# Layer 2's last norm of each pair applied to rows as they lie, and one stream's last statistics made by ScalarE

## The chip, the cores and the metric

One core of a Trainium2 chip. The metric is device microseconds of one execution. The kernel before takes 1713.87 us, median of three executions (1713.86 to 1713.9).

## What is computed

x has 8 items of 512 tokens by 512 features, all float32. The reference, cut to what matters:

```python
def _mingru(x, Wz, bz, Wh, bh):                     # Wz = Wh = ctx_1024[i], bz = bh = cond_1024[i]
    z = sigmoid(einsum('bsi,hi->bsh', x, Wz) + bz)
    h_tilde = tanh(einsum('bsi,hi->bsh', x, Wh) + bh)
    a = clip(1.0 - z, 1e-8, 1 - 1e-8)
    return _linear_scan(a, z * h_tilde)             # h[t] = a[t] * h[t-1] + z[t] * h_tilde[t]

def _stack(x, ...):
    h = x
    for i in range(4):                              # layers 0 to 3
        h_new = _mingru(h, ...)
        if i > 0: h_new = h_new + h
        h = _layernorm(h_new, gamma, beta)          # over the 512 features
    return h

x = x + concat(_stack(norm(x)), flip(_stack(flip(norm(x))))) @ fusion_W.T + fusion_b
x = x + layernorm(gelu(norm(x) @ ternary(W_fc).T)) @ ternary(W_proj).T
```

Each item has two directions, forward and backward, so that there are 16 streams of four layers. Both directions use the same weights; the backward one differs in that its scan runs from the end.

## The kernel before

**Layout.** The state of a stream, `state[s]`, is a tile of 128 partitions (features of one chunk) by 4 chunks by 512 tokens: features lie on the partitions, tokens along the row. That is what the gate matmuls and the scan along tokens want. The layernorm is over features, that is over partitions. So `norm` (line 340) turns each of the four token tiles with four transposes on TensorE into a PSUM bank `pt` (`turned`, line 316; pool `ps_t`, two banks), where a token has its features along the row. `stats` (line 168) makes mean and variance on VectorE (`bn_stats`, `bn_aggr`, and two small instructions for `ve`, the variance plus epsilon, and `nmu`, minus the mean), and GpSimd takes the power -0.5 (`rs`, line 178). ScalarE writes the normalised tokens `tok` from the bank (`nmr` and `tok`, lines 188 and 189). Then `back` (line 320) turns the four chunks back, four transposes each, into a bank `pf` (pool `ps_f`, two banks), and ScalarE writes the chunk into the state with gamma as scale and beta as bias (line 331).

Layer 3 has no turning back: its norm is folded into the fusion weights, and `norm_last` (line 354) makes only the statistics: four transposes into `pt`, `bn_stats`, `bn_aggr`, `ve`, and the power into `rsv`. The fusion scales its two products by `rsv` (line 609).

**Order.** The order on every engine is the order in which the program is written (`manual_schedule`). It is made of slots (`slot`, line 439). A slot first issues its own work, mostly the eight matmul instructions of one output chunk of a layer, into one of four banks `u` (`gates`, line 457; two instructions per float32 matmul), followed by three activations on ScalarE for `a`, `t` and `z` (lines 479 to 481). Then it takes what is due of other streams: one piece from `turns` (the turning and its statistics), one from `backs` (the turning back), and one each from `xturns` and `xbacks` (`x_shares`; these serve the norm of the input of the next pair, whose last step `scale_x` makes four transposes into a `ps_f` bank `pr` and a ScalarE copy, and in the last pair the norm before the feed-forward part, whose transposes go to a `ps_f` bank `py`). Then come clamp, product and scan of the slot on VectorE (lines 485, 490, 494), the additions that are due ("resid": in layer 3 the sums of line 571, one a slot), and at the very end the closures that the pieces returned, in the order of the shares (`last`). A closure registered as "late" for a later slot is run there before the shares.

`Tokens` counts the four tiles of a norm; the turning back is ready one slot after the fourth tile was appended. `held` counts tiles of the `tok` pool in use; turns wait while it is 10.

**Pairs.** Items go in pairs. The four streams of a pair b are here called A = (b, 0), B = (b, 1), C = (b+1, 0) and D = (b+1, 1). Layers 1 to 3 run as A, B, C, D of layer 1, then of layer 2, then of layer 3, four slots each; then comes the fusion of the two items, between whose slots layer 0 of the next pair is put. D is the last stream whose layer 2 ends. In what follows slot n is counted from the first slot of D's layer 2: slots 0 to 3 are D's layer 2, 4 to 7 A's layer 3, 8 to 11 B's, 12 to 15 C's, 16 to 19 D's, and from 20 on the fusion and the next layer 0. By the pauses in the code D's turning falls into slots 5 to 8 and its turning back into slots 9 to 12. The sums of A's layer 3 are in slots 7 to 10 and of B's in 11 to 14. A's last statistics are in slots 12 to 15, B's in 16 to 19, C's from 20 and D's from 24. The input norm of the next pair's first item has its statistics in slots 4 to 7 and `pr` in slot 9, that of the second item in slots 12 to 15 and 17. In the last pair there is no next pair; the four `py` are there instead, one a slot, from the second slot after their fourth token tile.

After the 16 streams the feed-forward part runs over 16 hidden chunks of each item.

Of the kernel before, what the change touches and what calls it, by code (L numbers as in the profile page):

```python
# [9 lines left out]
F32 = mybir.dt.float32  # L10
F32R = mybir.dt.float32r
AF = mybir.ActivationFunctionType
ALU = mybir.AluOpType
# [3 lines left out]
P = 128  # L17
LN_EPS = 1e-5
# [6 lines left out]
def kernel(  # L25
# [26 lines left out]
    nc = tc.nc  # L52
    B, S, H = x.shape
    L = gru_wT.shape[0]
    F = fc_wT.shape[1]
    NC_ = H // P
    NT = S // P
# [7 lines left out]
    small = ctx.enter_context(tc.tile_pool(name="small", bufs=8))  # L65
    wpool = ctx.enter_context(tc.tile_pool(name="wts", bufs=1))
    hp = ctx.enter_context(tc.tile_pool(name="h", bufs=6))
    dram = ctx.enter_context(tc.tile_pool(name="x1", bufs=1, space=bass.MemoryType.DRAM))

    tokp = ctx.enter_context(tc.tile_pool(name="tok", bufs=TOK))  # L70
    xsp = ctx.enter_context(tc.tile_pool(name="xs", bufs=12))
    zp = ctx.enter_context(tc.tile_pool(name="z", bufs=ZT))
    ps_f = ctx.enter_context(tc.tile_pool(name="ps_f", bufs=2, space=PSUM))
# [18 lines left out]
    xs = {}  # L92
# [15 lines left out]
    gam = const.tile([P, NC_], F32, name="gam")  # L108
    bet = const.tile([P, NC_], F32, name="bet")
# [11 lines left out]
    for i in range(2):  # L121
# [3 lines left out]
        s = fusp.tile([P, P], F32R, name=f"fpick{i}")  # L125
# [36 lines left out]
    ident = const.tile([P, P], F32, name="ident")  # L162
    make_identity(nc, ident)
    mhalf = const.tile([P, 1], F32, name="mhalf")
    nc.vector.memset(mhalf, -0.5)
    ngb = const.tile([P, L, NC_], F32, name="ngb")

    def stats(src, name, rs=None, shift=True):

        st = small.tile([P, 6], F32, tag="st", name=f"st_{name}")  # L170
        nc.vector.bn_stats(st, src)  # L171
        mv = small.tile([P, 2], F32, tag="mv", name=f"mv_{name}")
        nc.vector.bn_aggr(mv, st)  # L173
        if rs is None:
            rs = small.tile([P, 1], F32, tag="rs", name=f"rs_{name}")
        ve = small.tile([P, 1], F32, tag="ve", name=f"ve_{name}")
        nc.vector.tensor_scalar(ve, mv[:, 1:2], LN_EPS, None, ALU.add)
        nc.gpsimd.tensor_tensor(rs, ve, mhalf, ALU.pow)  # L178
        if not shift:
            return rs, None  # L180
        nmu = small.tile([P, 1], F32, tag="nmu", name=f"nmu_{name}")
        nc.vector.tensor_scalar(nmu, mv[:, 0:1], -1.0, None, ALU.mult)  # L182
        return rs, nmu

    def normalise(dst, src, rs_nmu, name):
        rs, nmu = rs_nmu
        nmr = small.tile([P, 1], F32, tag="nmr", name=f"nmr_{name}")
        nc.scalar.activation(nmr, nmu, AF.Copy, scale=rs)
        nc.scalar.activation(dst, src, AF.Identity, bias=nmr, scale=rs)  # L189
# [39 lines left out]
    with rec:  # L229
# [7 lines left out]
        now = [0]  # L237
        state = {}
        rsv = {}
        turns, backs = [], []  # L240

        held = [0]
# [32 lines left out]
        zlive = [0]  # L275

        left = {}

        def queue(q, key, at, piece, go):
            left[key] = left.get(key, 0) + 1  # L280
            q.append((at, piece, key, go))
# [6 lines left out]
        def need(*keys):  # L288

            while any(left.get(k) for k in keys):  # L290
                slot(None, 2)

        def tokens(source, tok, rs, name):

            def go():
                src = source()
                found = stats(src, name, rs, tok is not None)
                if tok is None:
                    return lambda: None
                held[0] += 1  # L300

                def last():
                    tile_ = tokp.tile([P, H], F32, tag="tok", name=f"tok_{name}")
                    normalise(tile_, src, found, name)
                    tok.append(tile_)
                return last
            return go

        def turned(zs, t, name, frees=0):
            def source():  # L310
                if t == NT - 1:
                    zlive[0] -= frees
                spare = name.startswith("00_0") and t > 1
                pt = (ps_f if spare else ps_t).tile([P, H], F32, tag="pf" if spare else "pt", name=f"pt_{name}")
                for c in range(NC_):
                    nc.tensor.transpose(pt[:, ts(c, P)], zs[c][:, ts(t, P)], ident)  # L316
                return pt
            return source
# [35 lines left out]
        def norm_last(s, tag):  # L354
            rsv[s] = small.tile([P, NT], F32, tag="rsv", name=f"rsv_{tag}")
            zs = [state[s][:, c, :] for c in range(NC_)]
            for t in range(NT):
                queue(turns, s, now[0] + NC_ + 1, t, tokens(turned(zs, t, f"{tag}_{t}"), None, rsv[s][:, t : t + 1], f"{tag}_{t}"))

        rx, scale = {}, {}  # L360

        def scale_x(b):
# [9 lines left out]
                return last  # L372
            return go

        def second(b, t):

            def go():
                src, name = xs["n", b, t], f"x{b}_{t}"
                sm, nm, ss, ve = (small.tile([P, 1], F32, tag=k, name=f"{k}_{name}") for k in ("sm", "nm", "ss", "ve"))
                nc.scalar.activation(src, src, AF.Copy, accum_out=sm)  # L380
                nc.scalar.activation(nm, sm, AF.Copy, scale=-1.0 / H)
                nc.scalar.activation(src, src, AF.Square, bias=nm, accum_out=ss)

                def end():
                    nc.vector.tensor_scalar(ve, ss, 1.0 / H, LN_EPS, ALU.mult, ALU.add)
                    nc.gpsimd.tensor_tensor(rx[b][:, t : t + 1], ve, mhalf, ALU.pow)
                stages.append((now[0] + 1, "late", end))
                return None if now[0] or b else end
            return go
# [33 lines left out]
        stages = []  # L423
# [15 lines left out]
        def slot(work=None, cap=1, long=False):  # L439

            end = work() if work is not None else None
            due("factors")
            due("late")
            due("clamps")
            if long:
                due("scans")
            last = shares(cap) + x_shares()
            due("scans")
            if end is not None:
                end()  # L450
            due("resid")
            for f in last:
                if f is not None:
                    f()
            now[0] += 1

        def gates(h, l, o, name, scans):

            def work():
                u = ps_u.tile([P, S], F32, tag="u", name=f"u_{name}")  # L460
                for c in range(NC_):
                    nc.tensor.matmul(  # L462
                        u, lhsT=gw[l][:, c, ts(o, P)], rhs=h[:, c, :],
                        start=(c == 0), stop=(c == NC_ - 1),
                    )
                z = zp.tile([P, S], F32, tag="z", name=f"z_{name}")
                zlive[0] += 1
                a, t = factors(u, z, l, o, name)

                def end():  # L470
                    product(a, z, t)
                    scans(a, z)
                return end
            return work
# [17 lines left out]
        def scan(dst, a, z, backward):  # L492
            d = slice(None, None, -1) if backward else slice(None)
            nc.vector.tensor_tensor_scan(dst[:, d], a[:, d], z[:, d], 0.0, ALU.mult, ALU.add)  # L494
# [59 lines left out]
        def layer(s, l):  # L554
            while s not in state:
                slot(None, 2)
            need(s)
            zs = []
            h = state[s]
            for o in range(NC_):  # L560
                def scans(a, z, o=o):
                    scan(z, a, z, s[1] == 1)
                    zs.append(z)
                    if l < L - 1:
                        nc.vector.tensor_tensor(z, z, h[:, o, :], ALU.add)  # L565
                    elif o == NC_ - 1:

                        for c in range(NC_):
                            def sums(c=c):
                                zlive[0] -= 1  # L570
                                nc.vector.tensor_tensor(h[:, c, :], zs[c], h[:, c, :], ALU.add)
                            stages.append((now[0] + c, "resid", sums))
                slot(gates(h, l, o, f"{s[0]}{s[1]}_{l}_{o}", scans))

                if s[0] < 2 and (l == L - 1 or o % 2) and len(extra) > 2 * NW or s == (B - 1, 1) and l == L - 1:
                    pieces(1)
            now[0] -= 1
            if l < L - 1:
                norm(s, zs, f"{s[0]}{s[1]}_{l}", 2)
            else:  # L580
                norm_last(s, f"{s[0]}{s[1]}_{l}")
            now[0] += 1
# [165 lines left out]
        end = take(xturns)  # L748
# [94 lines left out]
    for i in range(2):  # L843
# [5 lines left out]
        s = const.tile([P, P], F32R, name=f"pick{i}")  # L849
# [137 lines left out]
    for j in range(ends):  # L987
        b, k = divmod(j, NF)
        late = []
# [22 lines left out]
        at = 12 if b == 0 else 8  # L1012
# [57 lines left out]
```

## Time and profile before

| | |
|---|---|
| median of three executions | 1713.87 us |
| the profiled execution | 1714.24 us |
| its span, first to last instruction | 1712.0 us |
| TensorE matmul / VectorE / ScalarE / GpSimd busy | 99% / 85% / 63% / 13% |
| granted TensorE clock | 1.000 |
| one transpose on TensorE, busy (line 325) | 273 ns, four of them start to start 0.44 us |
| eight matmul instructions of a chunk (line 462), start to start | 3.44 us |
| `bn_stats` from PSUM (line 171) | 693 ns |
| scan (line 494) | 1227 ns |
| `nmr` and `tok` on ScalarE (lines 188, 189) | 295 and 778 ns |
| affine from PSUM on ScalarE (line 331) | 786 ns |

Busy time of TensorE matmuls overlaps from one instruction to the next, and 99% says only that something is always in the array. What a step costs on TensorE is read from the starts of the instructions around it. Lines of the timeline give start, length, engine, line, operation and tiles; consecutive equal ones are merged, with their number at the end; in brackets is the idle time before and what ended it.

### The profile page before, as it was taken

The page shows a single profiled execution, that of the slowest core. Times are in us where ns is not written, and L with a number is a line of the kernel's source. Part 1 is how long each engine was busy: PE and PEld are TensorE (multiplying, and loading weights), DVE is VectorE, ACT ScalarE, POOL GpSimd, SP SyncE. Part 2 cuts the span into 40 slices and gives each one's busy share as a digit, 9 for nine tenths or more (in the row PEclk, how much of TensorE's full clock was granted, in tenths as well). Part 3 has the DMA queues.
Part 4 walks back from the last instruction along what each step waited for, and adds up shares of the span by engine and source line. Part 5 has one row for each costly group of instructions (what it writes and reads, how often), then busy time and mean ns, then how long its engine had stood idle before and what let it go on. Part 6 is the DMA issues. An engine that isn't in the chain of part 4 may idle for free.

```text
span 1712.0 us, 19766 instructions
## 1 busy us (share of the span) xinstructions
PE 1701.1 (99%) x6440; PEld 1042.4 (61%) x6440; DVE 1453.2 (85%) x2859; ACT 1074.6 (63%) x1858; POOL 222.3 (13%) x342
## 2 busy tenths in 40 slices
PE   9999999999999999999999999999999999999999
PEld 5455554555555455555545555554688888888887
DVE  7999989889998998999899899996568768768877
ACT  5898873468886246888524688860366566666654
POOL 3111111111111111111111111110000000000000
PEclk9999999999999999999999999999999999999999
DMA  8002231150000125000012200202201101100100
GB/s 271 19 25 81 99 93 37 65 193 1 1 19 13 56 68 191 1 1 19 13 56 69 104 21 29 74 1 99 74 1 50 50 0 50 49 19 31 50 19 31
DMA packets 46598, 91.74 MB, mean 54 GB/s; under 512 B 5280, under 2 KB 5536, under 8 KB 45472
## 3 DMA queue, kind: packets, MB, share of 16 engines
q1 hardware_dynamic: 45488, 88.78, 15.3%
q10 hardware_dynamic: 1008, 1.70, 0.3%
q8 instruction: 51, 0.84, 0.2%
q14 instruction: 51, 0.42, 0.1%
HBM read 65.30 MB, written 25.17 MB: 53 GB/s over the span
## 4 chain that ended last, share of the span: by engine, by line
PE 79%; DVE 16%; ACT 2%; issue 1%; DMA 1%; POOL 0%; DVEq 0%; ACTq 0%
PE u L462 28%; PE po L909 14%; PE ph L882 14%; PE pu L599 10%; PE pt L316 5%; DVE z L494 4%; PE pf L325 4%; PE u L511 4%; DVE st L171 2%; DVE z L490 2%; DVE a L485 1%; DVE z L565 1%; DVE zf L494 1%; PE py L214 1%; DVE mv L173 1%
## 5 line engine op out<-in xcount | busy, mean ns | idle before, releaser
L462 PE MATMUL u<-xT,gw 128*128 128x512 f32 x768 | 345.5, 593 | 0.0
L462 PE MATMUL u<-h,gw 128*128 128x512 f32 x768 | 345.5, 592 | 0.0
L494 DVE TENSOR_TENSOR_SCAN z<-a,z 128x512 f32<-128x512 f32 x224 | 274.9, 1227 | 7.6
L462 PEld LDWEIGHTS u<-xT,gw 128*128 128x128 f32 x768 | 138.6, 190 | 138.7 <-issue 136.8
L462 PEld LDWEIGHTS u<-h,gw 128*128 128x128 f32 x768 | 138.6, 190 | 138.2 <-issue 138.0
L479 ACT ACTIVATE a<-u,ngb 128x512 f32<-128x512 f32 x192 | 131.6, 685 | 139.6 <-PE u L462 139.1
L178 POOL TENSOR_TENSOR rs<-ve,mhalf 128x1 f32<-128x1 f32 x192 | 122.3, 637 | 679.8 <-DVE nmu L182 663.2
L171 DVE BATCH_NORM_STATS2 st<-pt 128x6 f32<-128x512 f32 x256 | 177.3, 693 | 37.7 <-PE pt L316 37.3
L909 PE MATMUL po<-pwq,ghi 128*128 128x512 f32 x512 | 202.7, 396 | 0.0
L882 PE MATMUL ph<-yhi,fcq 128*128 128x512 f32 x512 | 199.7, 390 | 0.0
L909 PE MATMUL po<-pwq,glo 128*128 128x512 f32 x512 | 199.6, 390 | 0.0
L882 PE MATMUL ph<-ylo,fcq 128*128 128x512 f32 x512 | 199.4, 389 | 0.0
L886 ACT ACTIVATE g<-ph 128x512 f32<-128x512 f32 x128 | 76.4, 597 | 186.2 <-PE ph L882 186.2
L490 DVE TENSOR_TENSOR z<-z,t 128x512 f32<-128x512 f32 x224 | 153.5, 685 | 10.3 <-ACT z L481 10.1
L189 ACT ACTIVATE tok<-pt,nmr,rs 128x512 f32<-128x512 f32 x192 | 149.3, 778 | 6.4
L897 DVE TENSOR_TENSOR acc<-acc,g 128x512 f32<-128x512 f32 x112 | 77.3, 691 | 84.7 <-ACT g L886 83.8
L481 ACT ACTIVATE z<-u,gb 128x512 f32<-128x512 f32 x192 | 132.4, 689 | 0.0
L480 ACT ACTIVATE t<-u,gb 128x512 f32<-128x512 f32 x192 | 130.8, 681 | 0.0
L316 PEld LDWEIGHTS pt<-ident,z 128*128 128x128 f32 x640 | 78.8, 141 | 77.4 <-issue 47.7
L511 PE MATMUL u<-xT,gw 128*128 128x512 f32 x256 | 115.0, 593 | 1.2 <-DVE gw L744 0.8
L599 PE MATMUL pu<-fw,xT 128*128 128x512 f32 x256 | 115.2, 593 | 0.0
L599 PE MATMUL pu<-fw,h 128*128 128x512 f32 x256 | 115.1, 592 | 0.0
(158 smaller groups left out, 2569.2 us busy)
## 6 DMA issues: line engine op xcount, KB each, us to landing
xf<-in_x_dram SPq DMA_DIRECT2D x32, 256.0 KB, 5.6
x<-xf SPq DMA_DIRECT2D x32, 256.0 KB, 2.0
xy<-x SPq DMA_DIRECT2D x32, 256.0 KB, 4.2
xn<-in_x_dram SPq DMA_DIRECT2D x31, 256.0 KB, 4.5
out_dram<-xy SPq DMA_DIRECT2D x31, 256.0 KB, 2.0
xT<-in_xt_dram SPq DMA_DIRECT2D x7, 1024.0 KB, 7.4
fca<-in_fc_wT_dram SPq DMA_DIRECT2D x16, 256.0 KB, 3.0
pwa<-in_proj_wT_dram SPq DMA_DIRECT2D x16, 256.0 KB, 2.6
```

The lines of the kernel that those rows point to most:

```text
L171: nc.vector.bn_stats(st, src)
L189: nc.scalar.activation(dst, src, AF.Identity, bias=nmr, scale=rs)
L316: nc.tensor.transpose(pt[:, ts(c, P)], zs[c][:, ts(t, P)], ident)
L462: nc.tensor.matmul(u, lhsT=gw[l][:, c, ts(o, P)], rhs=h[:, c, :], start=(c == 0), stop=(c == NC_ - 1),)
L479: nc.scalar.activation(a, u, AF.Sigmoid, bias=ngb[:, l, o : o + 1], scale=-1.0)
L481: nc.scalar.activation(z, u, AF.Sigmoid, bias=gb[:, l, o : o + 1])
L490: nc.vector.tensor_tensor(z, z, t, ALU.mult)
L494: nc.vector.tensor_tensor_scan(dst[:, d], a[:, d], z[:, d], 0.0, ALU.mult, ALU.add)
L511: nc.tensor.matmul(u, lhsT=gw[0][:, c, ts(o, P)], rhs=xT[b][:, c, :], start=(c == 0), stop=(c == NC_ - 1),)
L599: nc.tensor.matmul(pu, lhsT=hs[d][:, c, ts(t, P)], rhs=fw[:, d * NC_ + c, :], start=(c == 0), stop=(c == NC_ - 1),)
L882: nc.tensor.matmul(ph, lhsT=w, rhs=ys[b][c][i], start=(c == 0 and i == 0), stop=(c == NC_ - 1 and i == 1),)
L909: nc.tensor.matmul(po[b][t], lhsT=part[:, ts(t, P)], rhs=pwq[k // NP_][:, k % NP_, :], start=(k == 0 and i == 0), stop=(k == NF - 1 and i ...
```

## The change

For D, in each of the four pairs, `norm` is replaced by `norm_flat` in layer 2. The turning and the statistics stay, in the same slots; `rs` and `nmu` of the four tiles go into the columns of two small tiles. No tokens are written. In the slot in which the turning back would begin, `over` spreads each of the two columns over all partitions with four transposes of a broadcast column, into two `ps_f` banks, and ScalarE copies both to SBUF (`nmu` first). Over the next four slots, one chunk each, GpSimd adds the spread `nmu` to the chunk as it lies, VectorE multiplies by the spread `rs`, and one slot later ScalarE applies gamma and beta in place.

For C, `norm_last` has its statistics made by ScalarE (`by_scalar`): an activation Copy with a running sum, a small one for minus the mean, an activation Square with that bias and a running sum, both in place in the PSUM bank, then `ve` on VectorE and the power on GpSimd one slot later. `two_passes` is taken out of `second`, which did the same for two tiles of the first input norms.

```diff
-    def stats(src, name, rs=None, shift=True):
+    def stats(src, name, rs=None, shift=True, nmu=None):
...
-        nmu = small.tile([P, 1], F32, tag="nmu", name=f"nmu_{name}")
+        if nmu is None:
+            nmu = small.tile([P, 1], F32, tag="nmu", name=f"nmu_{name}")
...
             for t in range(NT):
-                queue(turns, s, now[0] + NC_ + 1, t, tokens(turned(zs, t, f"{tag}_{t}"), None, rsv[s][:, t : t + 1], f"{tag}_{t}"))
+                source, name = turned(zs, t, f"{tag}_{t}"), f"{tag}_{t}"
+                queue(turns, s, now[0] + NC_ + 1, t, by_scalar(s, t, source, name) if s[0] % 2 and s[1] == 0 else
+                      tokens(source, None, rsv[s][:, t : t + 1], name))
+
+        def by_scalar(s, t, source, name):
+            def go():
+                src = source()
+                left[s] += 1
+                def last():
+                    end = two_passes(src, src, rsv[s][:, t : t + 1], name)
+                    def rest():
+                        end()
+                        left[s] -= 1
+                    stages.append((now[0] + 1, "late", rest))
+                return last
+            return go
+
+        def norm_flat(s, zs, tag, pause):
+            toks, at = Tokens(), now[0] + pause
+            cols = {k: small.tile([P, NT], F32, tag=f"flat_{k}", name=f"{k}_{tag}") for k in ("rs", "nmu")}
+            spread = {}
+            def statistics(t):
+                def go():
+                    src = turned(zs, t, f"{tag}_{t}")()
+                    stats(src, f"{tag}_{t}", cols["rs"][:, t : t + 1], nmu=cols["nmu"][:, t : t + 1])
+                    return lambda: toks.append(t)
+                return go
+            def shift(c):
+                nc.gpsimd.tensor_tensor(state[s][:, c, :], zs[c], spread["nmu"], ALU.add)
+                zlive[0] -= 1
+            def apply(c):
+                h = state[s][:, c, :]
+                nc.vector.tensor_tensor(h, h, spread["rs"], ALU.mult)
+                def last():
+                    nc.scalar.activation(
+                        h, h, AF.Identity, bias=bet[:, c : c + 1], scale=gam[:, c : c + 1],
+                    )
+                    left[s] -= 1
+                    if c == NC_ - 1:
+                        held[0] -= 2
+                stages.append((now[0] + 1, "late", last))
+            def over():
+                state[s] = hp.tile([P, NC_, S], F32, tag="h", name=f"h_{s[0]}{s[1]}")
+                held[0] += 2
+                banks = {}
+                for k, v in cols.items():
+                    banks[k] = ps_f.tile([P, S], F32, tag="pf", name=f"pf_{k}_{tag}")
+                    for t in range(NT):
+                        nc.tensor.transpose(banks[k][:, ts(t, P)], v[:, t : t + 1].broadcast_to([P, P]), ident)
+                left[s] += NC_
+                for c in range(NC_):
+                    stages.append((now[0] + 1 + c, "late", lambda c=c: shift(c)))
+                    stages.append((now[0] + 1 + c, "resid", lambda c=c: apply(c)))
+                def last():
+                    for k in ("nmu", "rs"):
+                        spread[k] = tokp.tile([P, S], F32, tag="tok", name=f"{k}s_{tag}")
+                        nc.scalar.copy(spread[k], banks[k])
+                return last
+            for t in range(NT):
+                queue(turns, s, at, t, statistics(t))
+            queue(backs, s, toks, 0, over)
...
+        def two_passes(src, dst, rs, name):
+            sm, nm, ss, ve = (small.tile([P, 1], F32, tag=k, name=f"{k}_{name}") for k in ("sm", "nm", "ss", "ve"))
+            nc.scalar.activation(dst, src, AF.Copy, accum_out=sm)
+            nc.scalar.activation(nm, sm, AF.Copy, scale=-1.0 / H)
+            nc.scalar.activation(dst, src, AF.Square, bias=nm, accum_out=ss)
+            def end():
+                nc.vector.tensor_scalar(ve, ss, 1.0 / H, LN_EPS, ALU.mult, ALU.add)
+                nc.gpsimd.tensor_tensor(rs, ve, mhalf, ALU.pow)
+            return end
...
-            if l < L - 1:
+            if l == L - 2 and s[0] % 2 and s[1] == 1:
+                norm_flat(s, zs, f"{s[0]}{s[1]}_{l}", 2)
+            elif l < L - 1:
                 norm(s, zs, f"{s[0]}{s[1]}_{l}", 2)
```

More of the change, by code (lines that the diff above doesn't have):

```diff
@@ L373, in scale_x @@
             return go
+        def two_passes(src, dst, rs, name):
[7 more added lines that the diff above has]
+            return end
         def second(b, t):
             def go():
[L378 to L386, printed above, removed]
+                src = xs["n", b, t]
+                end = two_passes(src, src, rx[b][:, t : t + 1], f"x{b}_{t}")
                 stages.append((now[0] + 1, "late", end))
```

## The prediction

> **What bounds the kernel now.** I read the busy shares and the chain first, then the timeline of TensorE around slots 8 to 12 of the second pair, then the other engines there.
>
> ```profile
> PE 1701.1 (99%) x6440; PEld 1042.4 (61%) x6440; DVE 1453.2 (85%) x2859; ACT 1074.6 (63%) x1858; POOL 222.3 (13%) x342
> ...
> PE 79%; DVE 16%; ACT 2%; issue 1%; DMA 1%; POOL 0%; DVEq 0%; ACTq 0%
> ```
>
> TensorE sets the time; VectorE has 16% of the chain, so it is close behind somewhere. Slots 8 to 12 start with their transposes at 516.91, 521.22, 525.71, 529.58 and 533.45:
>
> ```profile
> 516.91 0.60 PE L316 MATMUL pt<-ident,z 128*128 128x128 f32 x4
> 517.34 0.60 PE L325 MATMUL pf<-ident,tok 128*128 128x128 f32 x4
> 517.78 3.60 PE L462 MATMUL u<-h,gw 128*128 128x512 f32 x8
> 521.22 0.79 PE L325 MATMUL pf<-ident,tok 128*128 128x128 f32 x4
> 521.84 0.60 PE L367 MATMUL pr<-ident,rx 128*128 128x128 f32 x4
> 522.27 3.60 PE L462 MATMUL u<-h,gw 128*128 128x512 f32 x8
> 525.71 0.60 PE L325 MATMUL pf<-ident,tok 128*128 128x128 f32 x4
> ```
>
> Start to start, four transposes are 0.44 us and a chunk is 3.44, with no room between. In this code TensorE's time falls only by removed transposes and grows by each wait. ScalarE and VectorE around it:
>
> ```profile
> 525.91 0.69 ACT L479 ACTIVATE a<-u,ngb 128x512 f32<-128x512 f32 x1 [1.41 <-PE u L462]
> ...
> 527.79 0.69 DVE L490 TENSOR_TENSOR z<-z,t 128x512 f32<-128x512 f32 x1 [0.73 <-ACT z L481]
> ...
> 533.53 0.67 DVE L571 TENSOR_TENSOR h<-z,h 128x512 f32<-128x512 f32 x1
> 534.11 0.69 DVE L171 BATCH_NORM_STATS2 st<-pt 128x6 f32<-128x512 f32 x1
> ...
> 553.87 0.69 DVE L171 BATCH_NORM_STATS2 st<-pt 128x6 f32<-128x512 f32 x1
> ```
>
> ScalarE begins 0.20 us after a chunk ends (525.71); VectorE's product follows at +2.08. In slots 10 and 11 VectorE idles. From 534.11 it has no gap and falls behind: the tile turned at 549.38 gets its statistics only at 553.87. They end at 554.56; the bank is wanted again by the transposes at 557.56. That slack of 3.00 us, the same in the first three pairs, is all that VectorE may lose there before TensorE stops.
>
> **What each edit costs**, per pair; C, D and the slots as defined above.
>
> *D's turning back.* Gone: 16 transposes, 4 `nmr` (295 ns), 4 `tok` (778), 4 affines from PSUM. New: 8 transposes in slot 9, 2 ScalarE copies, 4 GpSimd additions, 4 VectorE products, 4 affines from SBUF. No DMA and no SP instruction moves. On TensorE alone: slot 9 has 0.87 for two spreads in place of 0.44 plus a 0.18 wait of the fourth transpose on `tok` (0.79 where 0.60 is usual); slots 10 to 12 lose 0.44 each.
>
> *The new wait.* There are two `ps_f` banks. In slot 9 both now hold spreads, and `pr` comes next on TensorE, in the same slot: it needs a bank whose reader, a ScalarE copy, stands behind `a`, `t` and `z` of this slot. Behind `pr` waits slot 10's chunk, and everything after. That such a wait does hold TensorE is seen in the last pair, where `py` wants the bank of the one before:
>
> ```profile
> 1126.81 0.66 PE L214 MATMUL py<-ident,tok_y 128*128 128x128 f32 x4 [0.36 <-DVE ylo L220]
> ```
>
> ScalarE after a chunk end X: `a` at X+0.20; the next operation after `a`, `t`, `z` at X+1.93 (527.64 for 525.71). The `nmu` copy is like `scale<-pr` (0.594): done at X+2.53; the `rs` copy about 0.50 later. TensorE is ready at X+0.87. So it waits 1.7 us if `pr` gets `nmu`'s bank, 2.2 if it gets `rs`'s. No row says which; `nmu` is free first, so I lean to 1.7 and keep 2.2. Slot 9: 0.87 + 1.7 + 0.44 = 3.03, now 1.05 (521.22 to 522.27): +1.98; slots 10 to 12: -1.31. Net +0.67 (or +1.17) in each of three pairs: +2.0 (+3.5).
>
> *Last pair.* No `pr`, but the first `py` falls into slot 9 too: D no longer takes `tok` buffers, so its fourth turning is no longer put off by `held` (it is now at 1117.67, a slot after the others) and the `py` begin a slot earlier. Transposes and waits of slots 7 to 13 (1109.48 to 1135.48) are 6.69 now, by the starts around them; then 0.87 + 0.87 + 1.31 + 0.44 + 0.44 + 0.87 + 0.44 = 5.24 plus the wait of 1.7 to 2.2: +0.25 to +0.75.
>
> *GpSimd additions.* No row has a two-input one of this size. Nearest: the clamp (line 485), one input, same tile: 0.61 alone, up to 1.62 beside VectorE. It also stretches VectorE:
>
> ```profile
> 22.33 1.22 DVE L494 TENSOR_TENSOR_SCAN zf<-a,z 128x512 f32<-128x512 f32 x1
> 23.47 1.57 DVE L494 TENSOR_TENSOR_SCAN z<-a,z 128x512 f32<-128x512 f32 x1
> ...
> 22.72 1.25 POOL L485 TENSOR_SCALAR a<-a 128x512 f32<-128x512 f32 x1
> ```
>
> The scan under the clamp takes 1.57 for 1.22: 0.34 lost. The four additions queue on GpSimd back to back from X+2.6 (523.8), nothing else being there until slot 12. VectorE's next product can't start before slot 10's `z`: 521.22 + 3.03 + 3.44 + 2.08 = 529.8. In these 6.0 us VectorE has 1.7 of its own (scan, sum), so 4.2 are free: four additions of up to 1.05 cost nothing even if they shut VectorE out, and about 0.4 more is idle in slot 10. I take zero; at 1.62 each the loss is 6.5 - 4.6 = 1.9 per pair.
>
> [...] The 0.34 above is a part of an instruction, not all of it. [...]
>
> *VectorE products.* Four of 0.69, 0.61 start to start, in slots 10 to 13. Slots 10 and 11 wait for ScalarE anyway, but slot 12's statistics follow slot 11's product: its chunk ends at 521.22 + 3.03 + 2 x 3.44 = 531.13, plus 4.53 (529.58 to 534.11 now), plus 0.61: 536.27, 2.16 later than 534.11. Slots 12 and 13 have no gap: +1.22. At 553.87 VectorE is 3.38 later, TensorE 0.67: it has fallen back 2.71 of the 3.00. No stall, by 0.3. With the other bank both shift by 0.5. Layer 3 of D reads its last chunk about 549.2; that affine, after the product at 547.3, ends about 548.3. Cover 0.9.
>
> *C's statistics.* VectorE loses 4 x (0.69 + 0.18 + the waits between) = about 4.1 from slot 20 on and keeps `ve`. ScalarE gains 4 x (0.62 + 0.19 + 0.20 + 0.72 + 0.19) = 7.7, by the rows of lines 380 to 382; it is 63% busy and idles there. The bank of the first tile is free about 2.1 after its transposes, asked for 3.9 after. So VectorE is then 0.7 earlier than now, and the waits that end its stretch, 0.22, 0.34 and 0.69 us before and in the `zf` transposes near 316, 614 and 913, can go: 0 to -1.3, taken -1.0.
>
> **Sum.** +2.0 + 0.25 - 1.0 = +1.3 with `nmu`'s bank, +3.3 with `rs`'s (0.5 more in each of four pairs). Leaning to the first, +2.0. The profiled execution is 1714.24 (span 1712.0 and 2.24 around), so 1716.2 for it; the median is 0.37 below: **1715.9**. A difference of 0.2% (3.4 us) is about what a measurement of this kernel can tell, so this is no change.
>
> **Rivals.**
> 1. *Slower: GpSimd's additions shut VectorE out.* From about 1.2 us each, what they take beyond the idle 4.6 eats the last 0.3 of slack, and in slot 18 TensorE waits for a `pt` bank. At 1.62: 1.9 - 0.3 = 1.6 in three pairs, +4.8 above the forecast: 1720.7. For it: the clamp's 1.62 and that an addition reads twice as much. Against: the idle stretch, made longer by the very wait in slot 9.
> 2. *Faster: `pr` and `py` don't wait*, because the bank is free or ScalarE copies earlier. Then slot 9 is 1.31 (+0.26), a pair -1.05, the last -1.45, with the -1.3 of the ends: -5.9, so 1708.0. Against: there are only two banks, and both are full.
> 3. *D's rows come late.* If layer 3 waited for the whole tile and not for its chunk, slot 16 (546.6) would wait for 548.3: 1.7 in three pairs, 1721.0. Against: at 47.5 chunks of a layer start while ScalarE still writes later chunks (line 331, 47.49 to 48.92).
>
> **Chances.** No change, 1714.5 to 1717.3: 0.46. Slower by over 3.4: rival 1 with the unfavourable bank and rival 3, 0.37. Faster: rival 2, 0.17. Leaving out only the far parts of rivals 1 and 2, the range is 1708 to 1721.
>
> **What would show it.** After the eight spreads in slot 9, an idle of 1.7 or 2.2 on TensorE before `pr`, ended by a ScalarE copy, and the same before one `py`. [...] In slot 18 transposes without a wait, VectorE's statistics ending 0.3 before. No `zf` waits at the ends. A wait in slot 16 or 18 makes me wrong upwards; no wait in slot 9, downwards.

## The result and the profile after

The changed kernel takes 1726.62 us, median of six executions (1726.46 to 1728.17), against 1713.88 for the kernel before on the same chip: 1.0076 times as long, 95% interval 1.0063 to 1.0089. It is 12.7 us slower, outside the predicted 1708 to 1721. The profiled execution took 1726.57 us (span 1724.8), 12.3 more than the profiled execution of before.

The page of the changed kernel, busy times and shares of the chain by engine:

```profile
PE 1701.2 (99%) x6408; PEld 1040.0 (60%) x6408; DVE 1460.6 (85%) x2843; ACT 1089.2 (63%) x1914; POOL 249.4 (14%) x358
...
PE 85%; DVE 11%; ACT 2%; issue 1%; DMA 1%; POOL 0%; DVEq 0%; ACTq 0%
```

TensorE has 32 transposes fewer and the same busy time. VectorE's busy time is 7.4 us longer. The chain doesn't say where the time went; the timeline of TensorE does. Slot 9 of the second pair, changed kernel:

```profile
525.81 0.60 PE L417 MATMUL pf_rs<-ident,rs 128*128 128x128 f32 x4
526.25 0.60 PE L417 MATMUL pf_nmu<-ident,nmu 128*128 128x128 f32 x4
528.38 0.65 PE L440 MATMUL pr<-ident,rx 128*128 128x128 f32 x4 [1.54 <-ACT nmus L426]
528.87 4.46 PE L539 MATMUL u<-h,gw 128*128 128x512 f32 x10
```

This is the predicted wait: `pr` stands for the bank whose reader is the copy of `nmu`. From start to start `pr` comes 1.70 us later than after four transposes (528.38 - 526.25 - 0.43), and slot 9 takes 3.06 (525.81 to 528.87) where 3.03 was predicted. All four pairs have it, the last with `py`.

Then slot 16, the first slot of D's layer 3 and of B's last turning. TensorE and VectorE of the changed kernel:

```profile
554.66 0.49 PE L317 MATMUL pt<-ident,h 128*128 128x128 f32 x3
...
556.83 0.67 DVE L648 TENSOR_TENSOR h<-z,h 128x512 f32<-128x512 f32 x1
...
557.55 0.33 PE L317 MATMUL pt<-ident,h 128*128 128x128 f32 x1 [2.39 <-DVE h L648]
557.71 5.29 PE L539 MATMUL u<-h,gw 128*128 128x512 f32 x8
```

Three transposes go through, and the fourth waits for VectorE: not for a `pt` bank, but for what it reads. The tile of B is turned chunk by chunk, and its fourth chunk gets its last sum at 556.83. The fourth transpose begins 0.05 us after that sum's end, 2.56 us later than it would have followed the third. Three pairs have this wait. The same place in the kernel before:

```profile
548.35 0.67 DVE L571 TENSOR_TENSOR h<-z,h 128x512 f32<-128x512 f32 x1
...
549.38 0.60 PE L316 MATMUL pt<-ident,h 128*128 128x128 f32 x4
```

The sum ends at 549.02, so the fourth transpose could have begun at 549.07; it began at 549.38 + 3 x 0.11 = 549.71. VectorE had 0.64 us to lose here, not the 3.00 of the bank two slots later.

The last line of slot 16 above shows a third loss: eight matmul instructions take 5.29 us instead of 3.60. The same stretch by windows (the column before the last two is the granted TensorE clock):

```profile
558.00:559.00 1.00, 1.00 (x3) 0.38 (x2) 0.93 (x4) 0.00 (x0) 0.42 (x1) 0.88 0.00 0
559.00:560.00 1.00, 1.00 (x2) 0.34 (x1) 0.93 (x5) 0.00 (x0) 0.54 (x2) 0.50 0.00 0
...
561.00:562.00 1.00, 1.00 (x3) 0.48 (x2) 1.00 (x2) 0.00 (x0) 0.00 (x0) 0.50 0.00 0
562.00:563.00 1.00, 1.00 (x5) 0.44 (x4) 0.97 (x3) 0.00 (x0) 0.00 (x0) 0.92 0.00 0
```

The clock is halved (0.50) from about 558.8 to 562.2, beginning 1.2 us after the fourth transpose's start, and the matmuls lose 1.69 us. The first pair has the same (1.70 us), the third not (1.00).

**The account**, by starts on TensorE: slot 9, 4 x 1.70 = +6.8; slot 16, 3 x 2.56 = +7.7; halved clock +3.4; one transpose at 678.30, +0.4; waits of before that are gone (slot 9's fourth transposes, the `zf` transposes near 316, 614 and 913, and `py`), -1.9; transposes saved, 32 x 0.11 = -3.5. Sum +12.9; the profiled executions differ by 12.3.

Last, GpSimd and VectorE under the additions, changed kernel:

```profile
528.41 5.12 POOL L394 TENSOR_TENSOR h<-z,nmus 128x512 f32<-128x512 f32 x3 [3.34 <-ACT nmus L426]
528.61 2.18 DVE L571 TENSOR_TENSOR_SCAN z<-a,z 128x512 f32<-128x512 f32 x1
530.71 1.69 DVE L648 TENSOR_TENSOR xT<-z,xT 128x512 f32<-128x512 f32 x1
...
542.05 0.55 POOL L178 TENSOR_TENSOR rsv<-ve,mhalf 128x1 f32<-128x1 f32 x1 [8.52 <-DVE ve L177]
543.05 0.66 POOL L178 TENSOR_TENSOR rx<-ve_x,mhalf 128x1 f32<-128x1 f32 x1 [0.45 <-DVE ve_x L177]
543.68 1.35 POOL L394 TENSOR_TENSOR h<-z,nmus 128x512 f32<-128x512 f32 x1
543.94 2.17 DVE L571 TENSOR_TENSOR_SCAN z<-a,z 128x512 f32<-128x512 f32 x1
```

Three additions run one after another in slots 9 and 10. The fourth is written in slot 13 and stands behind the two powers of slot 12, so that it falls into the stretch in which VectorE has no gap. The scans take 2.18 and 2.17 for 1.22, the sum 1.69 for 0.67: each is held by 0.95 to 1.02.

### The profile page after: what moved, and what is told of

It is laid out like the page before. It is cut to its first block, busy times and chain, and to the rows that moved or that the text cites. A ratio compares the mean times of both kernels' runs of the same rounds, so it can differ in the third digit from the quotient of the medians.

```text
span 1724.8 us, 19665 instructions
## 1 busy us (share of the span) xinstructions
PE 1701.2 (99%) x6408; PEld 1040.0 (60%) x6408; DVE 1460.6 (85%) x2843; ACT 1089.2 (63%) x1914; POOL 249.4 (14%) x358
## 4 chain that ended last, share of the span: by engine, by line
PE 85%; DVE 11%; ACT 2%; issue 1%; DMA 1%; POOL 0%; DVEq 0%; ACTq 0%
PE u L539 28%; PE po L988 14%; PE ph L961 13%; PE pu L678 13%; PE u L588 6%; PE pt L317 5%; PE pf L326 4%; DVE z L571 3%; DVE st L171 1%; DVE z L567 1%; DVE z L642 1%; PE py L215 1%; DVE a L562 1%; DVE mv L173 0%; DVE h L648 0%
## 5 line engine op out<-in xcount | busy, mean ns | idle before, releaser
L571 DVE TENSOR_TENSOR_SCAN z<-a,z 128x512 f32<-128x512 f32 x224 | 282.5, 1261 | 7.6
L171 DVE BATCH_NORM_STATS2 st<-pt 128x6 f32<-128x512 f32 x240 | 166.1, 692 | 33.4 <-PE pt L317 33.1
L190 ACT ACTIVATE tok<-pt,nmr,rs 128x512 f32<-128x512 f32 x176 | 136.9, 778 | 5.9
```

## The experiments

The question was which of the parts costs the time: the wait in slot 9, VectorE's lateness at the sum, or GpSimd's hold on VectorE. All ratios are to the kernel before, run beside.

**One half of the change at a time.** First only C's statistics on ScalarE:

```diff
-            if l == L - 2 and s[0] % 2 and s[1] == 1:
+            if False:
                 norm_flat(s, zs, f"{s[0]}{s[1]}_{l}", 2)
```

> The changed kernel with D's norm as before: only C's last statistics on ScalarE. If that half is free and gives VectorE back about 1 us a tile behind slot 20, the waits of 0.2 to 0.7 us in the zf transposes near 316, 614 and 913 us go and the time is 1712.6 to 1713.6 us, 0.3 to 1.3 under the 1713.88 of before. If ScalarE's 1.9 us a tile hold a pt bank or the next layer 0 up, it is over 1715.

1713.56 us against 1714.11, ratio 0.9997 (0.9987 to 1.0006): 0.55 us lower, within what can be told. Then only the flat norm:

```diff
-                queue(turns, s, now[0] + NC_ + 1, t, by_scalar(s, t, source, name) if s[0] % 2 and s[1] == 0 else
+                queue(turns, s, now[0] + NC_ + 1, t, by_scalar(s, t, source, name) if False else
```

> The changed kernel with C's last statistics on VectorE as before: only the flat norm of D. The waits of 1.7 us in slot 9 and 2.6 us in slot 16 stay as they are, so at least 1724. If ScalarE's statistics are worth what I took, VectorE is now about 4 us a pair more loaded behind slot 20 and the zf transposes wait about 1 us in three pairs: 1728 to 1730 us. If they are worth nothing, 1726.6 as the whole change.

1726.90, ratio 1.0074 (1.0059 to 1.0089), with the waits of 1.70 in slot 9 and 2.56 in slot 16. The loss is all the flat norm's, and the statistics are worth nothing beside it; the 1.0 us that the prediction gave them isn't there.

**Without GpSimd's additions** (the mean is not taken off; the product reads the layer's output directly):

```diff
-                nc.gpsimd.tensor_tensor(state[s][:, c, :], zs[c], spread["nmu"], ALU.add)
                 zlive[0] -= 1
...
-                nc.vector.tensor_tensor(h, h, spread["rs"], ALU.mult)
+                nc.vector.tensor_tensor(h, zs[c], spread["rs"], ALU.mult)
```

> The changed kernel without the four GpSimd additions: the mean is not taken off D's layer-2 rows; VectorE's product reads the scan's rows directly. Theory deadline (VectorE comes late to the last sum of B's layer 3, which slot 16's fourth transpose reads, by its own products and its later start; slack 0.7 us): the wait in slot 16 falls only from 2.6 to about 2.0 us, time 1723 to 1725.5. Theory port (GpSimd's additions, 1.3 to 2.2 us, block VectorE and make that wait): the wait falls under 0.5 and TensorE's clock stays full, 1715 to 1717.

**Without VectorE's products** (the rows are not scaled by `rs`):

```diff
-                nc.vector.tensor_tensor(h, h, spread["rs"], ALU.mult)
```

> The changed kernel without the four VectorE products: D's layer-2 rows are not scaled by the reciprocal deviation; the additions on GpSimd stay. Theory deadline: three of the products lie ahead of that last sum, 3 x 0.61 = 1.8 us; the wait in slot 16 falls from 2.6 to about 0.7, TensorE's clock no longer halves, time 1716.5 to 1719. Theory port: the additions still block VectorE, the wait stays at 2 or more, 1724 or more.

Without additions 1722.01, ratio 1.0046 (1.0031 to 1.0061); without products 1718.81, ratio 1.0027 (1.0017 to 1.0038); the clock is whole in both (1.000). The wait in slot 16, without additions and then without products:

```profile
554.91 0.33 PE L317 MATMUL pt<-ident,h 128*128 128x128 f32 x1 [1.88 <-DVE h L647]
```

```profile
553.17 0.33 PE L317 MATMUL pt<-ident,h 128*128 128x128 f32 x1 [1.03 <-DVE h L647]
```

By starts the wait is 2.56 with both, 2.04 without additions, 1.19 without products. So the products make the larger part of it, the additions 0.5 us, and some of it is there without the products. There the chunk of slot 11 ends 9.93 us after slot 9's transposes begin (522.80 to 532.73), against 8.36 before (521.22 to 529.58), and VectorE's stretch without a gap begins that much later, by 1.57. TensorE comes to slot 16's transposes only 0.69 later (551.65 - 522.80 = 28.85 against 549.38 - 521.22 = 28.16), because it has fewer transposes in between. That leaves VectorE 0.88 behind, and the fourth addition's 0.95 makes it 1.83, which is the slack of 0.64 and the wait of 1.19. With the slack of 0.64, VectorE's lateness without additions is 2.68 us. The prediction's own sum, in which additions cost nothing, was 2.71.

**The slack measured by itself.** In the kernel before, three VectorE instructions that change nothing are put ahead of the sums of B's layer 3:

```diff
                                 zlive[0] -= 1
+                                if s[0] % 2 == 0 and s[1] == 1 and c < NC_ - 1:
+                                    nc.vector.tensor_tensor(zs[c], zs[c], zs[c], ALU.max)
                                 nc.vector.tensor_tensor(h[:, c, :], zs[c], h[:, c, :], ALU.add)
```

> The kernel before, with three additional VectorE instructions of 512 elements in each pair (each takes the larger of a tile and itself, 0.61 us start to start, 1.83 in all), just ahead of the first three sums of B's layer 3. Nothing else is changed, so VectorE falls 1.83 us back with no change to TensorE, ScalarE or GpSimd. Deadline theory (the fourth transpose of slot 16 wants the last of these sums, 0.7 us of slack): a wait of about 1.1 us in slot 16 of three pairs, 1714.1 + 3.4 = 1717.5, between 1716.5 and 1718.5. Bank theory, as in the prediction (only the pt bank of slot 18 is near, 3.00 us of slack): no wait, 1714.1, between 1713.7 and 1714.8.

1720.93, ratio 1.0040 (1.0026 to 1.0054). No GpSimd addition, no spread and no ScalarE copy has been added here, and the wait is the same one:

```profile
551.08 0.49 PE L316 MATMUL pt<-ident,h 128*128 128x128 f32 x3
...
552.29 0.67 DVE L573 TENSOR_TENSOR h<-z,h 128x512 f32<-128x512 f32 x1
...
553.01 0.33 PE L316 MATMUL pt<-ident,h 128*128 128x128 f32 x1 [1.44 <-DVE h L573]
```

The bank theory would have left the time at 1714.1. VectorE comes to the last sum 2.24 us later against TensorE, so the added instructions cost about 0.75 each and not 0.61 (the sum that follows each one reads what it wrote; whether that is why, no run shows). 2.24 - 0.64 = 1.60 is the wait in all three pairs, 4.8 us. Most of the rest of the 6.9 came later (`zf` transposes 0.6, `py` in the last pair 0.7, slot 9 of the second pair 0.4), which the expectation had left out.

**Taking the waits away.** `pr` and `py` one slot later:

```diff
-            queue(xbacks, ("x", b), at + NT + (2 if scalar else 1), 0, scale_x(b))
+            queue(xbacks, ("x", b), at + NT + 2, 0, scale_x(b))
...
-            toks.lag = 2
+            toks.lag = 3
```

> The changed kernel, with pr and py issued one slot later, so that neither asks for a bank in the slot in which both banks are full. The wait of 1.70 us in slot 9 should go in all four pairs (-6.8). Deadline theory: VectorE, which was 1.4 us idle for that wait in slots 10 and 11, gains only about 1.4 of the 1.7, so the wait in slot 16 grows from 2.56 to about 2.85 in three pairs (+0.9), and a third halved clock window may come (+1.7): 1720.7, between 1719.8 and 1722.6. If instead the wait in slot 16 is a follower of the one in slot 9 (VectorE late only because TensorE was held), it goes too: below 1715.

The wait in slot 9 is gone in all pairs, and the median is 1726.80 (1724.45 to 1730.02), ratio 1.0075 (1.0062 to 1.0089): nothing gained. In slot 16 TensorE now waits

```profile
556.30 0.33 PE L317 MATMUL pt<-ident,h 128*128 128x128 f32 x1 [3.10 <-DVE h L648]
```

3.26 us by starts in place of 2.56. Slot 16's own chunk takes 0.32 more (548.96 to 552.71), waiting for a chunk of D that ScalarE writes late (`h`, line 402). In the last pair, where there had been no such wait, slot 16 has one of 1.66. That returns 3 x (0.70 + 0.32) + 1.66 = 4.7 of the 6.8. What is left, 2.1, is what the profiled execution gained; it is the quickest of the four (mean clock 0.998). In the others the mean clock was 0.994 to 0.997; in which stretches it was lower, no trace shows.

The wait in slot 9 had hidden a part of VectorE's delay. VectorE's clamp and product of slot 10, in the changed kernel and then with `pr` later:

```profile
533.23 0.58 DVE L562 TENSOR_SCALAR a<-a 128x512 f32<-128x512 f32 x1 [0.83 <-ACT a L556]
534.39 0.69 DVE L567 TENSOR_TENSOR z<-z,t 128x512 f32<-128x512 f32 x1 [0.58 <-ACT z L558]
```

```profile
531.80 1.49 DVE L562 TENSOR_SCALAR a<-a 128x512 f32<-128x512 f32 x1
533.21 0.68 DVE L567 TENSOR_TENSOR z<-z,t 128x512 f32<-128x512 f32 x1
```

The 1.41 us of idle time are gone, but the clamp now lies under the third addition and takes 1.49. So the product comes only 0.66 us earlier after the start of slot 9's transposes (533.21 - 525.29 against 534.39 - 525.81), while TensorE no longer waits 1.70. The first three additions cost nothing only as long as slot 9's wait gives VectorE that idle time. The expectation had seen 0.3 of the loss per pair, not 1.0, and not the last pair.

B's last turning one slot later, so that the fourth transpose asks for the last sum 3.9 us later:

```diff
-                queue(turns, s, now[0] + NC_ + 1, t, by_scalar(s, t, source, name) if s[0] % 2 and s[1] == 0 else
+                queue(turns, s, now[0] + NC_ + 1 + (s[0] % 2 < s[1]), t, by_scalar(s, t, source, name) if s[0] % 2 and s[1] == 0 else
```

> The changed kernel, with B's last turning begun one slot later, so that its fourth transpose wants the last sum of B's layer 3 a slot (3.9 us) later. Slot 9 is as in the changed kernel. Deadline theory: the waits of 2.56 in slot 16 and the halved clock behind two of them go: 1726.6 - 7.7 - 3.3 = 1715.6, between 1714.5 and 1717.5 (VectorE stays some 2.6 us farther behind than it was, which may bring tenths later). If VectorE is simply too slow for slots 12 to 19 and not for one deadline, the wait comes back in slot 17 or 18 and the time stays above 1722.

1720.38, ratio 1.0037 (1.0024 to 1.0049). The wait in slot 16 and the halved clock are gone (mean granted clock 1.000), but 1.45 us of waiting came back in slot 17, in three pairs, at `pr`, whose fourth column is a power that GpSimd makes from a VectorE statistic:

```profile
557.63 0.32 PE L440 MATMUL pr<-ident,rx 128*128 128x128 f32 x1 [1.28 <-POOL rx L178]
```

Neither branch of the expectation was right in full: the wait came back in slot 17, as the second had it, but smaller. The deadline was moved away, and the next one lay only 1.1 us behind it (2.56 - 1.45). Both shifts together:

> Both shifts, of pr and py and of B's last turning. If the two waits are all that the change costs, what remains are the transposes saved and the statistics on ScalarE: 1715.6 - 6.8 = 1708.8, between 1708 and 1711, which is faster than the kernel before (1714.1). If the wait in slot 9 is only moved to another place, between 1713 and 1716.

1715.22, ratio 1.0007 (0.9998 to 1.0016). Both waits are gone, and VectorE, still late, stops TensorE behind the fusion:

```profile
573.54 0.66 PE L317 MATMUL pt<-ident,xT 128*128 128x128 f32 x4 [1.39 <-DVE st L171]
```

1.56 us here and in the third pair. The wait moves from deadline to deadline as long as VectorE has too much to do between slot 10 and the next layer 0.

**Two ways to make VectorE earlier.** All additions issued at once, ahead of slot 12's powers:

```diff
-                    stages.append((now[0] + 1 + c, "late", lambda c=c: shift(c)))
+                    stages.append((now[0] + 1, "late", lambda c=c: shift(c)))
```

> The changed kernel with all four GpSimd additions issued together, right after the copies of the spreads, so that the fourth no longer stands behind slot 12's two powers and runs in slots 9 and 10 with the others. If the first three additions cost nothing (VectorE would have waited for ScalarE in slots 9 and 10 anyway) and only the fourth does (its scan took 2.17 in place of 1.22, in a stretch without a gap), the wait in slot 16 falls from 2.56 to about 2.0, as in the kernel without additions, and the halved clock goes with it: 1726.6 - 1.6 - 3.3 = 1721.7, between 1721 and 1723.5. If the idle time of slots 9 and 10 is used up by three, the fourth costs the same there: 1726.6, between 1724.5 and 1728.

1721.18, ratio 1.0042 (1.0028 to 1.0056). GpSimd runs all four in a row, and the wait is 1.97, no longer than without any addition:

```profile
526.35 6.52 POOL L394 TENSOR_TENSOR h<-z,nmus 128x512 f32<-128x512 f32 x4 [3.32 <-ACT nmus L426]
...
554.89 0.33 PE L317 MATMUL pt<-ident,h 128*128 128x128 f32 x1 [1.79 <-DVE h L648]
```

That it is no longer is partly chance: the fourth addition still costs 0.40 us here (slot 10's scan begins 7.13 us after `pr`, 533.45 - 526.32, where with three additions it was 6.73), and VectorE has short steps, described in the last section, which give as much back. One addition, a hold of 0.95 us in the wrong place, had cost 5.4 us in all, since behind the wait of 2.56 the clock was also halved in two of three pairs, and behind the one of 1.97 in none (mean 1.000).

ScalarE making the statistics of A's second and fourth tile too:

```diff
-                queue(turns, s, now[0] + NC_ + 1, t, by_scalar(s, t, source, name) if s[0] % 2 and s[1] == 0 else
+                queue(turns, s, now[0] + NC_ + 1, t, by_scalar(s, t, source, name) if s[1] == 0 and (s[0] % 2 or t % 2) else
```

> The changed kernel, in which ScalarE also makes the last statistics of A's second and fourth item tiles (slots 13 and 15). VectorE loses twice about 1.0 us, the first of them ahead of the third sum of B's layer 3 and the second behind the last one or just ahead of it; nothing is changed on TensorE. Deadline theory: the wait in slot 16 falls by 1.0 to 2.0, to 0.6 to 1.6 in three pairs, and the halved clock goes: 1726.6 - 3.0 (to 6.0) - 3.3 = 1717.3 to 1720.3. If it is ScalarE that is late in this stretch, nothing is gained: 1725 to 1728.

1719.82, ratio 1.0034 (1.0021 to 1.0048), the wait down by 0.95 to 1.61: one of the two tiles has its statistics ahead of the last sum, and it counts in full; the other comes after it. ScalarE isn't late. The same edit with both shifts, and on the norm of before:

> pr, py and B's last turning one slot later as in the run before last, and ScalarE making A's second and fourth last statistics. That run left waits for VectorE's statistics of 0.4, 1.6 and 1.6 us behind the fusion, 0.7 before the zf transposes, and 0.2 to 0.4 in slots 15 and 18. If VectorE's 98% busy stretch from slot 11 to the fusion is what held it, taking about 2.0 us of VectorE's work out of it takes most of these away: 1715.2 - 4.5 = 1710.7, between 1709.5 and 1713, faster than the kernel before (1714.1). If the waits have another cause: 1714.5 to 1716.

> The norm of layer 2 as before for all items, and ScalarE making C's last statistics and A's second and fourth. It shows what the statistics on ScalarE are worth where TensorE's order is that of before, with its waits of 0.13 in slot 9 and 0.15 at the zf transposes as all that VectorE can give back: 1713.5, between 1712.8 and 1714. If VectorE's load in slots 12 to 19 cost TensorE time before the change too, below 1712.5.

With both shifts 1710.07, ratio 0.9977 (0.9968 to 0.9986), faster than both kernels. Behind the fusion the transposes come almost without a wait (0.20 by starts):

```profile
570.43 0.66 PE L317 MATMUL pt<-ident,xT 128*128 128x128 f32 x4
```

On the norm of before the statistics alone give 1713.41, ratio 0.9996 (0.9987 to 1.0005): VectorE's load there cost TensorE nothing that can be told from noise. Between these two kernels lie 3.3 us, and 32 transposes fewer are 3.5. So the flat norm seems to be worth its transposes (the two shifts were not run on the norm of before), but only once both turnings have been moved and VectorE has been given the room: the shifts alone gave 1715.22, the room alone 1719.82.

## Why the prediction was wrong

**The step that failed** is "That slack of 3.00 us, the same in the first three pairs, is all that VectorE may lose there before TensorE stops." It was read from one releaser of the transposes, the statistics that free their output bank. The transposes also read a chunk that VectorE has just summed, and that edge had 0.64 us. In the changed kernel it cost 3 x 2.56 = 7.7 us of waiting and 3.4 by the halved clock. The two lines stood in the timeline of before, at 548.35 and 549.38. The lateness itself was right: 2.71 by the prediction, 2.68 by the run without additions. With the true slack the prediction's working ends at 1715.9 + 3 x (2.71 - 0.64) = 1722.1, and the kernel without additions, which is what this working describes, took 1722.01. Part of that agreement is luck: the forecast held 1.0 less for C's statistics and 0.7 more for a wait on the bank of `rs`, neither was there, and the two nearly cancel.

**The wait in slot 9** was right in place, cause and size (1.70 for 1.7, by `nmu`'s bank, in four pairs), and so was the last pair, where `py` met it.

**"I take zero" for GpSimd's additions** was half right. They hold VectorE by 0.95 to 1.02 us a time (in the run without them the same scans take 1.22 and the sum 0.67), not the 0.34 of the clamp's row, and take 1636 ns in the mean. The zero needed at most 1.15 each (the 4.2 and 0.4 us of idle time over four), and no row of before showed their length. Still the first three cost nothing in the changed kernel: counted from the start of `pr`, slot 10's scan begins 6.73 us later with them (535.11 - 528.38) and without them (532.99 - 526.26), since VectorE would have waited for ScalarE. Wrong was "back to back from X+2.6 (523.8), nothing else being there until slot 12": each addition is written in its own slot, and the fourth comes after slot 12's powers. In time the fourth addition goes on for 1.09 us after the scan's start (543.68 + 1.35 - 543.94), and the scan takes 0.95 more. The clamp's 0.34 was read from a shorter overlap: the clamp ended at 23.97 (22.72 + 1.25), the scan began at 23.47, so the two met only for 0.50 us, and of these the scan lost 0.34.

**C's statistics**, -1.0: measured -0.55 alone, within noise, and nothing in the changed kernel. By starts the three `zf` waits are 1.07 us before and 0.28 in the changed kernel, but two of the three are small with the flat norm alone as well (0.10, 0.10 and 0.51), and the transpose at 678.30 waits 0.4 more in the changed kernel.

**The clock** was no term of the sum. Idle time of TensorE was priced by its length alone, and two of three waits in slot 16 cost another 1.7 each (granted clock 0.50).

**The rivals.** None was it. Rival 1 had a true part, 0.5 us of the wait (2.56 with the additions, 2.04 without), and put it on the bank of slot 18; rival 3 named slot 16, but for ScalarE's rows, which did not stop TensorE in the changed kernel (with `pr` later they did, by 0.32). None of them doubted the slack of 3.00.

## What to carry to other kernels

Before work is moved onto an engine that has no gaps, list for each instruction that it could hold up all that this waits for, its inputs as well as its output buffer; the slack is the least of them, and one comfortable edge says nothing of the others (here 3.00 us at the bank and 0.64 at the sum). When one deadline is moved, the late engine can meet the next, as here, where 2.56 us in slot 16 became 1.45 in slot 17: what had to be changed was VectorE's load (1710.07 with it), not only the order (1715.22). And a wait removed from TensorE can gain little when another engine was catching up behind it: the 6.8 us of slot 9 went, and the median was 1726.80 for 1726.62.

## What had not been expected of the hardware

After an idle time of TensorE of 2.39 to 2.40 us in slot 16 of three pairs the granted clock of the changed kernel was 0.50 for 3.4 us in two of them (254.97 to 258.38 and 558.75 to 562.17) and stayed at 1.00 in the third. With `pr` later it was halved in the first and the third pair, from about 254.3 and 858.4, for 3.4 us each, and stayed at 1.00 behind the 3.10 us of the second. After 1.88 us and less, in the profiles without additions, without products and with all additions early, it was never halved (mean 1.000). So in these runs the length of the gap alone does not say whether the clock is halved. The halving also begins late: 0.65 us after the fourth transpose's start in the first pair of the changed kernel, 1.20 us after it in the second (254.32 and 557.55). What decides it, no run shows.

In slots 12 to 14 of the first three pairs VectorE's step from `bn_aggr` to `ve` took 0.28 to 0.29 us from start to start in the kernel before, without additions and without products, and 0.21 to 0.22 in the changed kernel and its other variants with both. Six of them lie ahead of the last sum, which gives back 0.4 us: so the fourth addition's 0.95 is seen as 0.5 in the wait. No run explains it.
